# A graph layer's gathers and sums: buffers filled in one direction, sums issued first, one-hots for two parts

## The chip, the cores and the metric

The kernel runs on one core of a Trainium2 chip. The metric is the device time of one execution in microseconds (us). A core has five engines with a queue of instructions each, worked off in order: TensorE (PE, with its weight loads as PEld), VectorE (DVE), ScalarE (ACT), GpSimd (POOL) and SyncE (SP). DMAs are issued from the queues of SP, ACT and POOL. A gather of rows by a list of indices (an indirect DMA) is issued here by POOL.

## The reference

A graph of 12500 nodes with 128 features and 200000 edges, sorted by the edge's target `dst`. Each edge has one of ten relations, the position of the greatest of ten of its attributes. Two layers are computed; the second has no ReLU, and the result is added to `x` and normalized by row.

```python
seg = dst * NUM_REL + edge_type
xs = x[src]
sums = segment_sum(xs, seg, num_segments=N * NUM_REL)
cnt = segment_sum(ones, seg, num_segments=N * NUM_REL)
mean = (sums / maximum(cnt, 1.0)[:, None]).reshape(N, NUM_REL, -1)
return einsum('nrd,rdo->no', mean, w_rel) + x @ root + bias
```

`edge_type = argmax(edge_attr[:, 16:26])`, `h = relu(layer(x))`, `out = layernorm(x + layer(h))`.

## The kernel before

**Tiles and parts.** The edges are cut into 1563 tiles of 128. Four tiles are a *part* (`QB` = 4); layer 1 has 391 parts. For each tile POOL gathers the 128 source rows (`gathered`, L825, the issue is L827). VectorE makes a one-hot matrix of 120 columns (`hots`, L830, L834): 12 nodes that the tile's edges can reach times ten relations, each edge's entry weighted by one over its count. PE multiplies rows and one-hot (`products`, L1063, L1070) into a PSUM bank; two tiles share a bank, and there are four banks (`fixed`). VectorE adds the bank's part of a tile to `cc` at an offset that is read into registers (`sum_into`, L857, the addition is L860). `cc` is a ring of 1024 nodes and an edge of 172; when the tiles cross its end, at tiles 10, 138, 266 and so on (every 128), ACT copies the edge to the front (`lap_begun`, L806 to L808).

**Both layers at once.** From tile 177 (`NX`) on, a gather takes two rows' worth for each edge from the table `TB`: the source's features and, if that node's first layer is already finished and written to `TB`, its projected row for layer 2 (`limit_of` says up to which node). Such a tile has a second product against a *node one-hot* of 12 columns without the relations (L1074). These node one-hots are made in `hots` as well, for the part's four tiles together: an equality into PSUM (`nodeP`, L838) and a product with the weights into the part's one-hot buffer (L840), each over 48 columns. Tiles before 177 are *plain*. What layer 1 could not take along is gathered in layer 2 (L1396), 177 tiles of the early edges and 687 of the later ones, which are brought together in lists on VectorE first.

**Buffers.** Six gather buffers of eight slots of 128 columns. Plain tiles take one slot, two parts to a buffer, and go round six buffers, after tile 48 round five. The others take two slots, a part to a buffer, round four (`NEAR`). Each time that a buffer is used again it is filled in the other direction (`turn`, L1048 to L1051): the slot filled first is then the one whose product ran last. The one-hots go round four buffers (`OB`), made one part ahead (`AHEAD`); the sums of a part come two parts behind its products (`BEHIND`).

**The order.** Layer 1 is written out by hand: each engine gets its instructions in the order of the loop at L1034. Iteration p issues:

1. VectorE: the one-hots of part p+1, the node one-hots among them;
2. POOL: the gathers of part p;
3. VectorE: the sums of tiles 0 and 1 of part p-2 (`sums(0, 2)`, L1077). If the part begins a group of 128 tiles, ACT first fetches a row of offsets by a DMA (L1085); if it begins a group of 16, VectorE loads 16 offsets into registers (L851);
4. PE: the products of tiles 0 and 1 of part p;
5. postponed work that is due (`todo.run`, L1107; `jobs.run`, L1108);
6. VectorE: the sums of tiles 2 and 3 of part p-2, with `lap_begun` on ACT where a lap begins, and then, where a block of nodes has all its edges, `finish` (L918): 20 matmuls that project the block by ten relations (`projected`, L820);
7. PE: the products of tiles 2 and 3, and once more `todo.run`.

`finish` puts its later steps into `todo`: one step later ACT takes the projection out of PSUM (`rows_copied`, L933, the instruction is L749), then the second layer's projections for each relation are made and written to `TB`, and the ring is cleared. `jobs` holds what the later tiles need: for each chunk of 128 tiles the relations, keys and weights (`prepared`, L651), the shifted indices (`shifted_rows`, L435, which also fills `nodeE` for the node one-hots), and the limits of the lists of layer 2: `tile_limits` (L475) runs 252 small instructions (L486), eight at a time, each next eight 8 tiles later, beginning at tile 320.

**The start.** ACT zeroes `cc` in pieces of 512 columns (L1128) while the first chunk is prepared; POOL gathers the first 48 tiles meanwhile.

Of the kernel before, what the change touches and what calls it, by code (L numbers as in the profile page):

```python
# [70 lines left out]
def rgcn_resnorm_kernel(ctx: ExitStack, tc: tile.TileContext, x, src, dst, attr, w_rel1, root1, b1,  # L71
# [145 lines left out]
    gathers = [lasting.tile([P, GQ * C], F32, name=f"g{i}") for i in range(GB)]  # L217
    hots_ = [lasting.tile([P, QB * KY], F32, name=f"oh{i}") for i in range(OB)]
    turn_of_ = {"g": 0, "oh": 0, "ys": 0}

# [113 lines left out]
    iotaP, riotaP, topP, kpP = in_bank(KW), in_bank(NREL), [in_bank(Q), in_bank(Q)], in_bank(P + 2 * L)  # L334
    nodeP = in_bank(QB * WN)
    nc.vector.tensor_copy(iotaP, columns[:, :KW])
# [98 lines left out]
    def shifted_rows(a, b, limit):  # L435

        first = NX // QB * QB if a == NX else a
# [37 lines left out]
    def tile_limits():  # L475
# [7 lines left out]
        for to, first in zip(reach_of, (low_of, high_of)):  # L483
            nc.vector.memset(to, 0.0)
            for i, t in enumerate(first):
                nc.vector.scalar_tensor_tensor(to, u, t - 0.5, to, op0=ALU.is_gt, op1=ALU.add)  # L486
                if i % 8 == 7:
                    yield 1
# [215 lines left out]

    zero = const.tile([P, YB], F32, name="zero")

# [122 lines left out]

    def hots(keys, weights, cols, n, m, nodes=None):  # L830

        oh = next_of("oh", hots_)
        for j in range(n):
            nc.vector.tensor_scalar(oh[:, j * m:(j + 1) * m], cols[:, :m], keys[:, j:j + 1], weights[:, j:j + 1],  # L834
                                    op0=ALU.is_equal, op1=ALU.mult)
        if nodes is not None:
            eq = nodeP[:, :n * WN].rearrange("p (t n) -> p t n", n=WN)
            nc.vector.tensor_tensor(eq, nodes[:, :, None].to_broadcast([P, n, WN]),  # L838
                                    cols[:, None, :WN].to_broadcast([P, n, WN]), op=ALU.is_equal)
            nc.vector.tensor_tensor(oh[:, QB * KW:QB * KW + n * WN].rearrange("p (t n) -> p t n", n=WN), eq,  # L840
                                    weights[:, :, None].to_broadcast([P, n, WN]), op=ALU.mult)
        return oh
# [61 lines left out]
    def layer_1():  # L904
# [118 lines left out]
        for n, a in enumerate(range(0, T0, 2 * G)):  # L1023
            jobs.at((92 + 2 * n) * QB, lambda t, a=a: by_relation(a, min(T0, a + 2 * G)))
        for i, a in enumerate(range(0, RW, YB)):
            def wipe(t, a=a):
                m = min(YB, RW - a)
# [3 lines left out]
        used = {}  # L1031
        turn_of_["zp"] = 0
        fixed = [ps_z.tile([P, YB], F32, name=f"zp{i}") for i in range(4)]
        for p in range(-AHEAD, NPT + BEHIND):  # L1034
            if p + AHEAD < NPT:
                t0, n = parts[p + AHEAD]
                ohs[p + AHEAD] = hots(keyE[:, t0:t0 + n], wE[:, t0:t0 + n], iotaP, n, KW,
                                       nodeE[:, t0 % NODES:t0 % NODES + n] if t0 + n > NX else None)
            if p < 0:
                continue  # L1040
            t = p * QB
            if p < NPT:
                t0, n = parts[p]
                plain = t0 + n <= NX
                if not plain or p % 2 == 0:
                    g = next_of("g", (gathers if t < GB * GQ else gathers[:-1]) if plain else gathers[:NEAR])
                if not plain or p % 2 == 0:
                    turn = used[id(g)] = 1 - used.get(id(g), 1)  # L1048
                slot = [p % 2 * QB + j if plain else 2 * j for j in range(n)]
                if turn:  # L1050
                    slot = [GQ - (1 if plain else 2) - a for a in slot]  # L1051
                for j in range(n):
# [4 lines left out]
                    else:  # L1057
                        gathered(g, slot[j], TB[:N + NREL * limit_of(i)], idx, 2)
                made = (g, ohs.pop(p), slot)
            if p == NPT - CP // 4:  # L1060
                xbs[NBLK - 1] = rows_in(NBLK - 1)
                fTs[NBLK - 1] = features_in(NBLK - 1, 0, xbs[NBLK - 1])
            def products(g, oh, slot, a, b):  # L1063
                n = parts[p][1]
                for j in range(a, min(b, n)):
# [6 lines left out]
                    if i >= NX:  # L1072
                        a = QB * KW + j * WN
                        nc.tensor.matmul(zp[:, o + KW:o + KY], g[:, (slot[j] + 1) * C:(slot[j] + 2) * C], oh[:, a:a + WN],  # L1074
                                         start=True, stop=True)

            def sums(a, b):  # L1077
                nonlocal done, offs, row
                q = p - BEHIND
                if q < 0:  # L1080
                    return
                t0, n = parts[q]
                if not a and t0 % CT == 0:
                    row = rows_.tile([1, CT], I32, name="row")
                    nc.scalar.dma_start(row, b_r[t0 // CT:t0 // CT + 1, :])  # L1085
                if not a and t0 % G == 0:
                    m = min(G, NT - t0)
                    offs = offsets(row[:, t0 % CT:t0 % CT + m], t0, m, bounds)
                for j in range(a, min(b, n)):
                    i = t0 + j  # L1090
                    if i and lap_of_tile(i) > lap_of_tile(i - 1):
                        lap_begun()
                        if lap_of_tile(i) * RN < lap:
                            todo.at(t + 3 * QB, lambda _: edge_cleared())
                    sum_into(NS if i >= NX else NREL, zps[q, j // 2], j % 2 * KY, offs[i % G], WN)
                    if j % 2 or j == n - 1:
                        del zps[q, j // 2]
                if b < QB:
                    return
                while done < NBLK and t0 + n >= done_after(done):  # L1100
                    finish(done, t)
                    done += 1

            if p < NPT - 1:
                sums(0, 2)
                products(*made, 0, 2)
                todo.run(t - QB // 2)  # L1107
                jobs.run(t)  # L1108
                sums(2, QB)
                products(*made, 2, QB)  # L1110
            else:
                jobs.run(t)
                sums(0, QB)
                if p < NPT:
# [10 lines left out]
    flat = cc[:, :NREL].rearrange("p r n -> p (r n)")  # L1125
    for a in range(0, NREL * RW, YB):
        m = min(NREL * RW - a, YB)
        nc.scalar.activation(flat[:, a:a + m], zero[:, :m], AF.Copy)  # L1128
# [603 lines left out]
```

## Time and profile before

| | us |
|---|---|
| median of 3 runs | 3123.92 |
| lowest and highest | 3121.44, 3126.94 |
| the profiled execution, its own time | 3128.32 |
| its span in the profile | 3126.5 |
| busy: PE, DVE, ACT, POOL | 2155.1, 2118.9, 370.3, 2296.7 |
| issue of the first and of the last gather | 4.1, 3105.8 |

The span runs from the first instruction to the end of the last; the execution's own time is a little longer. Busy time of POOL is that of its instructions; a gather's data arrive later than its instruction ends. In a timeline each row has a start, a duration, the engine, the line, and in square brackets the engine's idle time ahead of it with what ended it. In a table of waits, a row tells who waited for whom: the sum in us, how often, the longest.

### The profile page before, as it was taken

How to read it: one execution, taken by the hardware profiler on the slowest of the kernel's cores; microseconds unless marked ns; L12 is line 12 of the kernel's file. 1: busy time of each engine (PE TensorE's matmuls, PEld its weight loads, DVE VectorE, ACT ScalarE, POOL GpSimd, SP SyncE). 2: the span in 40 equal slices, each digit the busy share in tenths (PEclk: the TensorE clock that was granted, in tenths of full speed). 3: DMA queues.
4: the chain of work that ended last, by engine and by line, in shares of the span. 5: the costliest groups of instructions: out<-in, count | busy, mean ns of one | idle time of the engine just before them, and what ended most of it. 6: DMA issues, size and time to landing. Idle time of an engine off the chain costs nothing.

```text
span 3126.5 us, 37701 instructions
## 1 busy us (share of the span) xinstructions
PE 2155.1 (69%) x10120; PEld 1783.0 (57%) x10120; DVE 2118.9 (68%) x8089; ACT 370.3 (12%) x602; POOL 2296.7 (73%) x2439
## 2 busy tenths in 40 slices
PE   2768787877878787888888888843655555555554
PEld 1546666666767676767676767743554444444443
DVE  6868688888777877777776868479773443434443
ACT  1112111111111111111111111100000000000000
POOL 6777777676777777777777777777777777777775
PEclk8778777776878777777777868855755555555555
DMA  6676667575666666666666655532222222222222
GB/s 183 184 216 185 200 184 232 160 215 158 200 193 196 197 194 197 196 196 196 196 185 192 184 159 146 142 94 60 60 60 63 66 70 66 67 66 70 66 67 56
DMA packets 444103, 454.59 MB, mean 145 GB/s; under 512 B 53110, under 2 KB 376239, under 8 KB 443880
## 3 DMA queue, kind: packets, MB, share of 16 engines
q0 software_dynamic: 99840, 250.04, 28.9%
q1 hardware_dynamic: 303331, 182.87, 19.6%
q10 hardware_dynamic: 40709, 19.15, 2.1%
q8 instruction: 85, 1.39, 0.2%
q14 instruction: 138, 1.13, 0.1%
HBM read 309.45 MB, written 148.80 MB: 147 GB/s over the span
## 4 chain that ended last, share of the span: by engine, by line
DVE 30%; POOL 20%; PE 19%; issue 15%; DMA 11%; DVEq 3%; ACT 1%; SPq 0%; POOLq 0%; ACTq 0%
POOL g L827 20%; DVE oh L834 8%; DVE cc L860 7%; PE pf L820 7%; DMA g<-TB,idxE 5%; PE zp L1070 4%; DVEq L851 3%; DMA g<-TB,idxB 2%; PE yb L949 2%; DMA row<-b_r 2%; PE zp L1074 2%; DVE bank L838 1%; DVE reach L486 1%; DVE acc L1554 1%; DVE cc L1274 1%
## 5 line engine op out<-in xcount | busy, mean ns | idle before, releaser
L827 POOL DMA_INDIRECT g<-TB,idxE x1563 | 1478.6, 946 | 525.8 <-issue 421.2
L1070 PE MATMUL zp<-oh,g 128*128 128x120 f32 x3126 | 822.6, 361 | 367.0 <-DVE cc L860 258.3
L1070 PEld LDWEIGHTS zp<-oh,g 128*128 128x128 f32 x3126 | 601.8, 235 | 523.9 <-DVE cc L860 354.5
L827 POOL DMA_INDIRECT g<-TB,idxB x687 | 649.1, 945 | 209.3 <-issue 199.0
L860 DVE TENSOR_TENSOR cc<-cc,zp 128x132 f32 (+1 forms) x1563 | 453.0, 290 | 373.5 <-PE zp L1074 140.7
L1529 PE MATMUL zy<-oh,g 128*128 128x12 f32 (+23 forms) x1170 | 320.3, 380 | 314.0 <-DMA g<-TB,idxB 211.5
L1074 PEld LDWEIGHTS zp<-oh,g 128*128 128x128 f32 x2772 | 529.7, 238 | 0.0
L834 DVE TENSOR_SCALAR oh<-bank,keyE,wE 128x120 f32<-128x120 f32 x1563 | 517.1, 392 | 0.0
L1529 PEld LDWEIGHTS zy<-oh,g 128*128 128x128 f32 x1170 | 274.3, 310 | 370.4 <-DMA g<-TB,idxB 230.5
L1074 PE MATMUL zp<-oh,g 128*128 128x12 f32 x2772 | 481.6, 249 | 0.0
L820 PE MATMUL pf<-cc,w 128*128 128x256 f32 (+2 forms) x1040 | 306.9, 466 | 6.3 <-DVE cc L860 5.9
L949 PE MATMUL yb<-w,a 128*128 128x512 f32 (+1 forms) x576 | 288.2, 583 | 2.3 <-ACT g L955 1.2
L820 PEld LDWEIGHTS pf<-cc,w 128*128 128x128 f32 x1040 | 250.1, 255 | 55.2 <-issue 5.8
L1529 PE MATMUL zq<-oh,g 128*128 128x16 f32 (+27 forms) x558 | 168.1, 395 | 155.6 <-DMA g<-TB,idxB 141.4
L1529 PEld LDWEIGHTS zq<-oh,g 128*128 128x128 f32 x558 | 138.2, 314 | 188.6 <-DMA g<-TB,idxB 154.2
L827 POOL DMA_INDIRECT g<-in_x_dram,idxE x177 | 167.4, 946 | 74.3 <-issue 50.6
L777 DVE TENSOR_TENSOR cc<-pf,cc 128x256 f32<-128x256 f32 (+2 forms) x52 | 21.2, 409 | 264.4 <-PE pf L1472 264.3
L1554 DVE TENSOR_TENSOR acc<-acc,zy 128x12 f32 (+25 forms) x585 | 104.3, 178 | 105.3 <-PE zy L1529 50.7
L834 DVE TENSOR_SCALAR oh<-columns,keyB,wB 128x15 f32<-128x15 f32 (+25 forms) x687 | 163.8, 322 | 0.1
L783 ACT ACTIVATE rstd<-mv,eps 128x2 f32<-128x2 f32 (+2 forms) x52 | 15.3, 295 | 967.1 <-DVE mv L781 967.0
L749 ACT ACTIVATE a<-pf,b 128x256 f32<-128x256 f32 (+1 forms) x50 | 23.3, 466 | 852.9 <-PE pf L822 852.9
L800 ACT ACTIVATE cc<-zero 128x1280 f32<-128x1280 f32 x90 | 118.8, 1368 | 4.8 <-DVE acc L942 4.8
(265 smaller groups left out, 1807.3 us busy)
## 6 DMA issues: line engine op xcount, KB each, us to landing
TB<-xb SPq DMA_DIRECT2D x88, 640.0 KB
m<-in_edge_attr_dram SPq DMA_DIRECT2D x48, 672.0 KB
TB<-g SPq DMA_DIRECT2D x98, 256.0 KB
g<-TB,idxE POOLq DMA_INDIRECT x1563
TB<-ys SPq DMA_DIRECT2D x96, 256.0 KB
g<-TB,idxB POOLq DMA_INDIRECT x687
TB<-ys SPq DMA_DIRECT2D x49, 128.0 KB
TB<-in_x_dram ACTq DMA_DIRECT2D x12, 512.0 KB
```

The costliest lines, as they stand in the source:

```text
L486: nc.vector.scalar_tensor_tensor(to, u, t - 0.5, to, op0=ALU.is_gt, op1=ALU.add)
L800: nc.scalar.activation(cc[:, r, o:o + n], zero[:, None, :n].to_broadcast([P, m, n]), AF.Copy)
L820: nc.tensor.matmul(po[:, :n], wsb[l][:, r, :], sums[:, r], start=(r == 0), stop=(w is None and r == NREL - 1))
L827: nc.gpsimd.indirect_dma_start(out=g[:, j * C:(j + n) * C], out_offset=None, in_=table, in_offset=bass.IndirectOffsetOnAxis(ap=idx, axis=0))
L834: nc.vector.tensor_scalar(oh[:, j * m:(j + 1) * m], cols[:, :m], keys[:, j:j + 1], weights[:, j:j + 1], op0=ALU.is_equal, op1=ALU.mult)
L851: vals = nc.values_load_multi_w_load_instructions(row, engines=[DVE], min_val=min(a for a, _ in lims), max_val=max(b for _, b in lims), sk ...
L860: nc.vector.tensor_tensor(s, s, zp[:, at:at + m * w].rearrange("c (r n) -> c r n", n=w), op=ALU.add)
L949: nc.tensor.matmul(yb[:h, :m], fin_a[k][:, b * P:b * P + h], wsb[1][:, r:r + m // C, :], start=True, stop=True)
L1070: nc.tensor.matmul(zp[:, o:o + KW], g[:, slot[j] * C:(slot[j] + 1) * C], oh[:, j * KW:(j + 1) * KW], start=True, stop=True)
L1074: nc.tensor.matmul(zp[:, o + KW:o + KY], g[:, (slot[j] + 1) * C:(slot[j] + 2) * C], oh[:, a:a + WN], start=True, stop=True)
L1529: nc.tensor.matmul(zp[:, j * w:(j + 1) * w], g[:, at * C:(at + 1) * C], oh[:, j * w:(j + 1) * w], start=True, stop=True)
L1554: nc.vector.tensor_tensor(s, s, zps[q][:, j * w:(j + 1) * w], op=ALU.add)
```

## The change

- Plain buffers are always filled from the front; the alternation stays for the others.
- A part's sums are taken out of the middle of the iteration: tiles 0 and 1 come before the one-hots of part p+1, tiles 2 and 3 between these and the node one-hots, all of them ahead of `todo.run` and `jobs.run`. `finish` stays where it was (`finished`).
- The node one-hots have buffers of their own (`nhots_`, two of 96 columns) and are made for two parts at once, in every other iteration (`node_hots`).
- `tile_limits` issues four instructions at a time, each next four 16 tiles later.
- `zero` has 256 columns instead of 512, and what copies from it takes pieces of 256.

```diff
-    hots_ = [lasting.tile([P, QB * KY], F32, name=f"oh{i}") for i in range(OB)]
+    hots_ = [lasting.tile([P, YB], F32, name=f"oh{i}") for i in range(OB)]
+    nhots_ = [lasting.tile([P, 2 * QB * WN], F32, name=f"nh{i}") for i in range(2)]
...
-                if i % 8 == 7:
+                if i % 4 == 3:
                     yield 1
...
-    zero = const.tile([P, YB], F32, name="zero")
+    zero = const.tile([P, BN], F32, name="zero")
...
+    def node_hots(t0):
+
+        n = min(2 * QB, NT - t0)
+        a = t0 % NODES
+        oh = next_of("nh", nhots_)
+        eq, to = [b[:, :n * WN].rearrange("p (t n) -> p t n", n=WN) for b in (nodeP, oh)]
+        nc.vector.tensor_tensor(eq, nodeE[:, a:a + n, None].to_broadcast([P, n, WN]),
+                                iotaP[:, None, :WN].to_broadcast([P, n, WN]), op=ALU.is_equal)
+        nc.vector.tensor_tensor(to, eq, wE[:, t0:t0 + n, None].to_broadcast([P, n, WN]), op=ALU.mult)
         return oh
...
-        jobs.job(80 * QB, tile_limits(), 2 * QB)
+        jobs.job(80 * QB, tile_limits(), 4 * QB)
...
         for p in range(-AHEAD, NPT + BEHIND):
+            t = p * QB
+            if 0 <= p < NPT - 1:
+                sums(p, t, 0, 2)
             if p + AHEAD < NPT:
                 t0, n = parts[p + AHEAD]
-                ohs[p + AHEAD] = hots(keyE[:, t0:t0 + n], wE[:, t0:t0 + n], iotaP, n, KW,
-                                       nodeE[:, t0 % NODES:t0 % NODES + n] if t0 + n > NX else None)
+                ohs[p + AHEAD] = hots(keyE[:, t0:t0 + n], wE[:, t0:t0 + n], iotaP, n, KW)
+            if 0 <= p < NPT - 1:
+                sums(p, t, 2, QB)
+            if p + AHEAD < NPT and t0 + QB > NX // (2 * QB) * 2 * QB and t0 % (2 * QB) == 0:
+                nhs[(p + AHEAD) // 2] = node_hots(t0)
...
-                if not plain or p % 2 == 0:
+                if not plain:
                     turn = used[id(g)] = 1 - used.get(id(g), 1)
-                slot = [p % 2 * QB + j if plain else 2 * j for j in range(n)]
-                if turn:
-                    slot = [GQ - (1 if plain else 2) - a for a in slot]
+                slot = [p % 2 * QB + j if plain else 2 * (n - 1 - j if turn else j) for j in range(n)]
...
             if p < NPT - 1:
-                sums(0, 2)
                 products(*made, 0, 2)
                 todo.run(t - QB // 2)
                 jobs.run(t)
-                sums(2, QB)
+                finished(p, t)
                 products(*made, 2, QB)
...
-    for a in range(0, NREL * RW, YB):
-        m = min(NREL * RW - a, YB)
+    for a in range(0, NREL * RW, BN):
+        m = min(NREL * RW - a, BN)
         nc.scalar.activation(flat[:, a:a + m], zero[:, :m], AF.Copy)
```

More of the change, by code (lines that the diff above doesn't have):

```diff
@@ L435, in shifted_rows @@
     def shifted_rows(a, b, limit):
-        first = NX // QB * QB if a == NX else a
+        first = NX // (2 * QB) * 2 * QB if a == NX else a
         m, f, _ = relations_of(first, b)
@@ L828, in gathered, with hots @@
                                      in_offset=bass.IndirectOffsetOnAxis(ap=idx, axis=0))
-    def hots(keys, weights, cols, n, m, nodes=None):
+    def hots(keys, weights, cols, n, m):
         oh = next_of("oh", hots_)
@@ L835, in hots @@
                                     op0=ALU.is_equal, op1=ALU.mult)
[L836 to L841, printed above, removed]
+        return oh
+    def node_hots(t0):
[6 more added lines that the diff above has]
+        nc.vector.tensor_tensor(to, eq, wE[:, t0:t0 + n, None].to_broadcast([P, n, WN]), op=ALU.mult)
         return oh
@@ L1059, in layer_1 @@
                 made = (g, ohs.pop(p), slot)
+                nh = nhs.get(p // 2)
             if p == NPT - CP // 4:
@@ L1072, in products @@
                     if i >= NX:
-                        a = QB * KW + j * WN
-                        nc.tensor.matmul(zp[:, o + KW:o + KY], g[:, (slot[j] + 1) * C:(slot[j] + 2) * C], oh[:, a:a + WN],
+                        a = (i % (2 * QB)) * WN
+                        nc.tensor.matmul(zp[:, o + KW:o + KY], g[:, (slot[j] + 1) * C:(slot[j] + 2) * C], nh[:, a:a + WN],
                                          start=True, stop=True)
[L1077 to L1102, printed above, removed]
             if p < NPT - 1:
-                sums(0, 2)
                 products(*made, 0, 2)
@@ L1112, in layer_1 @@
                 jobs.run(t)
-                sums(0, QB)
+                sums(p, t, 0, QB)
+                finished(p, t)
                 if p < NPT:
```

38 lines of the change are left out of this document (33 added, 5 removed).

## The prediction, made before the changed kernel ran

> **What bounds the kernel now.** I read the page first, then the table of busy time by stage, then in the stage that loses time the waits and the groups of VectorE (DVE), and last the timeline around single stalls.
>
> ```profile
> span 3126.5 us, 37701 instructions
> L827 POOL DMA_INDIRECT g<-TB,idxE x1563 | 1478.6, 946 | 525.8 <-issue 421.2
> ```
>
> Every gather is one POOL instruction of 946 ns with an idle stretch before it that nothing ends ("issue"). There are 1563 in layer 1 and 864 in layer 2, 2427 in all, one after another on one queue. Whether that queue is the bound is read from the stages (columns: window, length, then busy time and count of PE, PEld, DVE, ACT, POOL, then clock, DMA share, GB/s):
>
> ```profile
> 50.00:100.00 50.00, 16.89 (x58) 12.98 (x58) 42.29 (x154) 1.49 (x3) 23.63 (x26) 0.50 0.48 141
> ...
> 350.00:800.00 450.00, 348.65 (x1765) 290.10 (x1765) 371.15 (x1458) 72.72 (x106) 313.11 (x332) 0.75 0.64 190
> 800.00:1700.00 900.00, 742.66 (x3835) 626.92 (x3836) 686.55 (x2475) 155.44 (x228) 679.28 (x719) 0.77 0.66 195
> 1700.00:1750.00 50.00, 40.98 (x210) 33.31 (x211) 42.66 (x140) 7.75 (x13) 33.90 (x36) 0.80 0.56 160
> ...
> 1850.00:1950.00 100.00, 87.43 (x448) 70.51 (x448) 79.15 (x279) 18.01 (x27) 72.91 (x78) 0.81 0.50 140
> 1950.00:2050.00 100.00, 74.00 (x452) 63.70 (x452) 47.76 (x179) 15.36 (x35) 73.35 (x79) 0.83 0.56 153
> 2050.00:3100.00 1050.00, 545.19 (x1952) 447.36 (x1953) 552.74 (x2390) 20.77 (x66) 794.07 (x841) 0.52 0.26 65
> ```
>
> In the last row POOL issues 841 gathers in 1050 us, 1.249 us each, and its busy share is 794.07/1050 = 0.756. I take that share as the floor of a stage in which POOL never waits; busy time divided by 0.756 is the time that the stage's gathers need, and the rest of the window is lost. By this the windows lose: 50 to 100: 50 - 31.2 = **18.8**; 350 to 800: 450 - 414 = **36**; 800 to 1700: 900 - 898 = **1.8**; 1700 to 1750: **5.2**; 1850 to 1950: **3.6**; 1950 to 2050: **3.0** us. The sum, 68, is all that a change that leaves the gathers as they are can win: layer 2 and two thirds of layer 1 already run at POOL's pace.
>
> Who holds POOL up between 350 and 800 us:
>
> ```profile
> PE zp L1070 <- DVE cc L860: 87.4, 65, 6.5
> ...
> POOL g L827 <- PE zp L1074: 36.6, 17, 7.6
> ```
>
> A gather waits for the products that last read its buffer; the products wait for VectorE's sums (L860), which empty the PSUM banks. PE is idle for 450 - 348.65 = 101 us there, and 87 of them are that wait. So VectorE is the bound of this stage. Its groups in the window (count | busy, mean ns | idle before):
>
> ```profile
> L834 DVE TENSOR_SCALAR oh<-bank,keyE,wE 128x120 f32<-128x120 f32 x328 | 108.2, 392 | 0.0
> L860 DVE TENSOR_TENSOR cc<-cc,zp 128x132 f32 x329 | 95.8, 291 | 55.5 <-issue 25.2 <-ACT cc L808 6.9 <-PE zp L1074 6.4
> L486 DVE SCALAR_TENSOR_TENSOR reach<-u,reach 128x6 f32<-128x6 f32 x252 | 42.2, 167 | 7.6
> ...
> L838 DVE TENSOR_TENSOR bank<-nodeE,bank 128x48 f32<-128x48 f32 x82 | 17.4, 213 | 2.8
> L840 DVE TENSOR_TENSOR oh<-bank,wE 128x48 f32<-128x48 f32 x82 | 17.0, 207 | 2.8
> ```
>
> All 252 instructions of the list limits (L486) fall into this window, 49.8 us with their gaps, more than the 36 us that POOL loses.
>
> **The change part by part.**
>
> *List limits at a quarter of the pace.* Eight per 8 tiles become four per 16. In this window tiles 320 to about 617 pass: 297/16 = 18.6 steps of 4 instructions of 167 + 30 = 197 ns are 14.6 us in place of 49.8: -35.2. The other 35 us go to tiles 617 to 1344.
>
> *Node one-hots for two parts at once.* Two instructions over 96 columns replace four over 48. No row shows 96, so the price comes from two groups of the same operation:
>
> ```profile
> L860 DVE TENSOR_TENSOR cc<-cc,zp 128x132 f32 x1386 | 404.1, 292 | 336.4 <-PE zp L1074 139.0 <-issue 107.3 <-ACT cc L808 30.8
> ...
> L1554 DVE TENSOR_TENSOR acc<-acc,zy 128x12 f32 x177 | 29.4, 166 | 7.8 <-issue 1.4 <-PE zq L1529 0.7 <-DVE acc L1554 0.6
> ```
>
> (292 - 166)/120 = 1.05 ns a column, so 48 more cost 50 ns: 262 and 257 ns. The bounds are 212 (columns cost nothing) and 424 (no saving); I take the slope. Here 82 pairs of instructions (34.4 busy + 5.6 idle = 40.0 us) become 41 of 262 + 257 + 68 ns of gaps, 24.1 us: -15.9.
>
> *Sums ahead.* This has three effects. First, at a lap's turn:
>
> ```profile
> 1694.72 0.48 ACT L749 ACTIVATE a<-pf,b 128x256 f32<-128x256 f32 x1 [17.28 <-PE pf L822]
> 1695.10 1.77 ACT L808 ACTIVATE cc<-cc 128x1892 f32<-128x1892 f32 x1
> ```
>
> ```profile
> 222.43 0.59 DVE L860 TENSOR_TENSOR cc<-cc,zp 128x120 f32 x2 [7.33 <-ACT cc L808]
> ...
> 379.24 0.62 DVE L860 TENSOR_TENSOR cc<-cc,zp 128x132 f32 x2 [6.91 <-ACT cc L808]
> ...
> 890.23 0.62 DVE L860 TENSOR_TENSOR cc<-cc,zp 128x132 f32 x2 [0.84 <-ACT cc L808]
> ...
> 1696.90 0.62 DVE L860 TENSOR_TENSOR cc<-cc,zp 128x132 f32 x2 [6.72 <-ACT cc L808]
> ...
> 1860.63 0.62 DVE L860 TENSOR_TENSOR cc<-cc,zp 128x132 f32 x2 [7.03 <-ACT cc L808]
> ```
>
> The copy of the ring's edge (L808) stands on ACT behind L749, which waits for the 20 matmuls of a block's projection; the next sum waits for the copy. The four long waits are the laps at which a block ends in the part just before (tiles 136, 264, 1288, 1416). Once the sums of a part are issued ahead of the postponed work, L808 stands ahead of L749 and the projection is no longer in this chain; 0.84 us, as at the lap of 890 us where no block interferes, should stay. The stalls that end at 379, 1697 and 1861 us stand just before or in the windows in which POOL loses.
>
> Second, the row of offsets, once per 128 tiles:
>
> ```profile
> 1027.10 0.50 ACTq L1085 DMA_DIRECT2D row<-b_r  x1
> ...
> 1029.54 1.33 DVE L834 TENSOR_SCALAR oh<-bank,keyE,wE 128x120 f32<-128x120 f32 x4
> ...
> 1035.43 0.62 DVE L860 TENSOR_TENSOR cc<-cc,zp 128x132 f32 x2 [4.08 <-issue]
> ```
>
> ```profile
> 1027.10 5.87 DMA row<-b_r
> ```
>
> The row takes 5.87 us and VectorE has the one-hots (1.8 us, from 1029.54) to do meanwhile. Now it meets the wait first, with those one-hots queued behind it and PE behind the one-hots: a **loss**, bounded by 0 (ACT issues earlier) and 1.8 us a row. I take 1.8: three rows in this window, +5.4. The Trainium skill, "DMA: Bandwidth & Descriptors", section "Latency and other measured facts", puts a DMA's fixed cost at about 2 us, mostly the trip to memory, which the section says shrinks when the memory is lightly loaded. By that estimate the row would have landed at 1029.1, before VectorE comes, and the term would be 0; the 5.87 us row contradicts it here.
>
> Third, a part's sums no longer stand behind the jobs of the same iteration, so PE gets its second bank sooner. I count this at nothing; it is cover for the loss just named.
>
> VectorE's balance from 350 to 800 us: 450 - 35.2 - 15.9 - 6.1 (lap) + 5.4 = 398 us, under the 414 that POOL needs. So POOL becomes the bound here too. What stays lost is bounded by 0.8 us (the rate of 800 to 1700) and 36 (no effect). Busy VectorE time is 371.2 less 29.8 (178 of the 252 limits at 167 ns) less 13.1 (34.4 to 41 x 0.519) = 328 in 414 us, 79%, against 686.55/900 = 76% in the better stage; so I take 6, near the better stage: **-30**.
>
> *Plain buffers in one direction.* The start:
>
> ```profile
> 73.67 0.59 DVE L860 TENSOR_TENSOR cc<-cc,zp 128x120 f32 x2 [5.11 <-issue]
> ...
> 74.31 1.21 PE L1070 MATMUL zp<-oh,g 128*128 128x120 f32 x4 [23.30 <-DVE cc L860]
> ...
> 81.65 1.21 PE L1070 MATMUL zp<-oh,g 128*128 128x120 f32 x4 [1.52 <-DVE cc L860]
> ...
> 83.14 0.94 POOL L827 DMA_INDIRECT g<-in_x_dram,idxE  x1 [19.06 <-PE zp L1070]
> ```
>
> Gather 48 is the first that reuses a buffer, that of tiles 8 to 15. Filled from the other end, it takes tile 15's slot first and waits for the product that runs at 81.65 (tiles 14 and 15). Filled from the front it needs tile 8's, at 74.31: 8.9 us earlier, and each later slot has been read by the time that POOL comes to it at 1.25 us a gather, while PE takes two tiles in 1.7 to 2.9 us. Hoped 8.9, at worst 0 if VectorE cannot keep up with the earlier gathers; the lap stall before 222 us goes, which gives it 6.5 us back, so I take **-8.5**.
>
> *Late stages.* 1700 to 1750 and 1850 to 1950 keep 0.8 us each of 5.2 and 3.6: **-7.2**. From 800 to 1700 the list limits add 45 x 4 x 0.197 = 35.5 us, the nodes take 91 x 0.39 = 35.5 away, and six rows cost 10.8: POOL's loss goes from 1.8 to 4, **+2.2** (bounds: -1.8 and +26, 5.6 rounds at the worst price of the first rival). Layer 2 is not touched: 0.
>
> *Zeroing in halves* doubles ACT's instructions at the start; they end by 16.3 us and ACT then has nothing to do:
>
> ```profile
> 10.16 6.07 ACT L1128 ACTIVATE cc<-zero 128x512 f32<-128x512 f32 x12 [1.76 <-issue]
> 46.01 0.38 ACT L733 ACTIVATE fT<-pf 128x256 f32<-128x256 f32 x1 [29.78 <-PE pf L732]
> ```
>
> Nothing; twice the time would still be hidden in the 29.8 us.
>
> **Sum**: -30 - 8.5 - 7.2 + 2.2 = -43.5. The profiled execution took 3128.32 us (span 3126.5), which gives 3084.8. The median of the runs, 3123.92, is 4.4 lower: **3080**.
>
> **Rivals.**
> 1. *The peaks move on.* In every round of 128 tiles the row wait and the slower list limits put 1.8 + 2.8 us on VectorE before the ring of gather buffers is fullest (some 56 tiles in, 3.5 steps of 0.79) and the nodes take 2.7 off. That is 1.9 us a round, or 4.6 if the wider one-hots save nothing. If the early sums give nothing back, each of eight rounds from 350 to 1700 loses some 3 us: 24 less gain, 3104. For it: POOL's 1.8 us show that the ring is just full today. Against it: the third effect.
> 2. *PE holds the heavy stage.* It is busy 348.65 of 450 us. Then only the start, the laps and the late stages are won, 8.5 + 5 + 7.2: 3103. Against it: 87 of PE's 101 idle us are waits for VectorE.
> 3. *Slower.* VectorE now stands at the head of every part before the sums, with 1.33 us of one-hots behind them that it did before while PE finished. It waited for PE 86.3 us in 180 parts from 800 to 1700:
>
> ```profile
> DVE cc L860 <- PE zp L1074: 86.3, 46, 4.6
> DVE cc L860 <- issue: 62.5, 31, 6.5
> ```
>
> That is 0.48 us a part which can be absorbed, and perhaps 0.14 more, so a part that meets the new wait loses 0.71. It takes 61 of layer 1's 347 later parts to eat the gain; one part in three gives 82 - 43.5, about 3162. Against it: only 46 waits in 180 parts, and they come when VectorE is ahead.
> 4. *Nothing comes of it*: the earlier start is given back and rivals 1 and 2 act together: 3122.
>
> **How the numbers follow.** Forecast (3066 to 3092) 0.62; rival 1 0.20; rival 2 0.08; rival 3 0.06; rival 4 0.04. The low end is all of 36 + 8.8 + 1.8 + 8.9 us won: 3068, and 2 for the scatter of runs. The high end takes in rivals 1 and 2: 3106. About 0.2%, 6 us, is what a measurement here can tell from no change: faster 0.90, same 0.04, slower 0.06.
>
> **What would show it.** Gather 48 at 74 to 75 us; POOL near 0.756 busy from 350 on; L838 and L840 gone, two groups of 173 at about 260 ns in their place; list limits spread to about 1700 us; no wait of some 7 us for L808; the row's wait grown from 4 to about 6 us. If VectorE waits for PE in far more parts, rival 3 is at work; if POOL's waits return every 160 us, rival 1.

## The result and the profile after

The changed kernel takes 3092.51 us (median of 4 runs, 3089.70 to 3093.74), the kernel before in the same group 3123.75 us (4 runs, 3121.44 to 3126.94): a ratio of 0.9898, 95% interval 0.9881 to 0.9915. The forecast was 3080 (3066 to 3106, with 3066 to 3092 for the prediction's own account). The profiled execution after took 3089.7 us.

The page of the kernel after, and its table of busy time by stage (columns as before). The gathers cost what they cost before; the lines have moved: the gather is now L828, the one-hot L835, the sum L866, the copy of the ring's edge L809, the product L1111 and the product with the node one-hots L1115.

```profile
span 3087.4 us, 37680 instructions
L828 POOL DMA_INDIRECT g<-TB,idxE x1563 | 1478.3, 946 | 497.4 <-issue 420.6
```

```profile
50.00:100.00 50.00, 15.81 (x57) 12.75 (x58) 41.15 (x145) 1.86 (x5) 31.10 (x34) 0.50 0.48 144
...
250.00:350.00 100.00, 83.42 (x464) 71.18 (x463) 72.48 (x262) 19.62 (x30) 73.61 (x78) 0.83 0.67 196
350.00:800.00 450.00, 366.04 (x1902) 311.53 (x1901) 342.96 (x1261) 77.13 (x112) 334.86 (x355) 0.76 0.69 204
800.00:1700.00 900.00, 741.10 (x3829) 636.25 (x3828) 679.72 (x2491) 155.31 (x227) 676.19 (x716) 0.75 0.66 194
1700.00:1750.00 50.00, 45.09 (x258) 37.73 (x256) 37.44 (x133) 9.79 (x16) 37.84 (x40) 0.86 0.62 179
1850.00:1950.00 100.00, 89.63 (x504) 75.85 (x505) 64.09 (x225) 15.26 (x30) 75.63 (x80) 0.84 0.53 148
1950.00:2050.00 100.00, 64.64 (x342) 55.24 (x340) 57.93 (x188) 13.23 (x34) 72.28 (x76) 0.69 0.45 119
2050.00:3060.00 1010.00, 521.18 (x1845) 425.96 (x1845) 516.61 (x2291) 17.52 (x54) 763.59 (x809) 0.52 0.26 65
```

The last row is again the pace of an undisturbed POOL: 763.59/1010 = 0.756. Read with it as in the prediction (window less POOL's busy time over 0.756), POOL loses, beside what the forecast left it:

| window, us | before | forecast | after |
|---|---|---|---|
| 50 to 100 | 18.8 | 10.3 | 8.9 |
| 250 to 350 | 0 | 0 | 2.6 |
| 350 to 800 | 36 | 6 | 7.1 |
| 800 to 1700 | 1.8 | 4 | 5.6 |
| 1700 to 1750 | 5.2 | 0.8 | 0 |
| 1850 to 1950 | 3.6 | 0.8 | 0 |
| 1950 to 2050 | 3.0 | 3.0 | 4.4 |

The losses sum to 28.6 us against 68.4 before: 39.8 less, and the spans differ by 39.1. So the whole gain is POOL's lost time coming back.

Where VectorE was the bound, from 350 to 800 us, its groups after are these (count | busy, mean ns | idle before):

```profile
L866 DVE TENSOR_TENSOR cc<-cc,zp 128x132 f32 x358 | 103.1, 288 | 91.8 <-PE zp L1115 60.8 <-issue 22.3 <-ACT cc L809 1.8
...
L487 DVE SCALAR_TENSOR_TENSOR reach<-u,reach 128x6 f32<-128x6 f32 x76 | 12.8, 169 | 2.0
L847 DVE TENSOR_TENSOR nh<-bank,wE 128x96 f32<-128x96 f32 x44 | 11.3, 258 | 1.5
L845 DVE TENSOR_TENSOR bank<-nodeE,bank 128x96 f32<-128x96 f32 x44 | 11.2, 255 | 0.0
```

Of the 252 list limits only 76 are left in the stage. Ninety-six columns cost 255 ns (L845, the equality) and 258 ns (L847, the product with the weights), where 48 cost 213 and 207: 48 columns more cost 42 and 51 ns. The sums run as before. VectorE's idle time ahead of the sums has turned round: 60.8 of 91.8 us is now waiting for PE, where it was 6.4 of 55.5. Its opposite, PE waiting for the sums, is in the table of waits of the same window (sum in us, times, longest):

```profile
PE zp L1111 <- DVE cc L866: 33.6, 21, 3.7
```

```profile
POOL g L828 <- PE zp L1115: 11.6, 14, 5.4
```

21 waits instead of 65, 33.6 us instead of 87.4, and POOL's waits for the products are 11.6 us instead of 36.6. (Each of POOL's 14 contains the usual 0.3 us between two gathers, so 7.4 us of them are loss.)

The start, and two of the places where POOL still loses:

```profile
71.58 0.59 DVE L866 TENSOR_TENSOR cc<-cc,zp 128x120 f32 x2 [4.92 <-issue]
```

```profile
73.28 0.94 POOL L828 DMA_INDIRECT g<-in_x_dram,idxE  x1 [9.14 <-PE zp L1111]
...
541.85 0.94 POOL L828 DMA_INDIRECT g<-TB,idxE  x1 [5.41 <-PE zp L1115]
...
1349.16 0.94 POOL L828 DMA_INDIRECT g<-TB,idxE  x1 [2.56 <-PE zp L1115]
```

The first sum starts at 71.58 instead of 73.67 us, and gather 48 at 73.28 instead of 83.14 us. The other two gathers shown are 416 and 1056. Between 350 and 1700 us POOL loses at the gathers 416, 544, 672 and so on to 1184, and nearly nowhere else: 128 apart, always 32 tiles into a group of 128. How such a loss comes about is seen some 34 us earlier, in the timeline of 1314 to 1353 us:

```profile
1317.97 0.28 DVE L287 CAST idxE<-pf 128x128 int32<-128x128 f32 x1
...
1324.09 0.62 DVE L866 TENSOR_TENSOR cc<-cc,zp 128x132 f32 x2 [5.83 <-PE pf L989]
...
1324.62 1.33 DVE L835 TENSOR_SCALAR oh<-bank,keyE,wE 128x120 f32<-128x120 f32 x4
1324.76 0.50 PEld L1111 LDWEIGHTS zp<-oh,g 128*128 128x128 f32 x2 [1.18 <-DVE cc L866]
...
1330.76 0.78 PE L1111 MATMUL zp<-oh,g 128*128 128x120 f32 x2 [2.35 <-DVE cc L866]
```

```profile
1340.35 7.31 PE L821 MATMUL pf<-cc,w 128*128 128x256 f32 x20
```

VectorE reaches the sums of the group's first part at 1318.2 and sits idle for 5.83 us. The view names PE, but the chain of waits, followed back, has the row of offsets, fetched at 1315.34:

```profile
1315.34 6.03 DMA row<-b_r
1321.40 2.50 DVEq L857
```

The row lands at 1321.37, the register load takes it until 1323.90, and the sum starts at 1324.09. The one-hots of the next part, 1.33 us of VectorE, come only then, and whatever else VectorE has to do comes behind them, the later sums too. PE waits for sums, which empty its banks: 0.78 us at 1324.76 and 2.35 us at 1330.76. It is the same in the whole stretch from 350 to 1700 us, where PE's weight loads for the products wait 127.2 us for sums and 4.8 us for one-hots (sum in us, times, longest):

```profile
PEld zp L1111 <- DVE cc L866: 127.2, 102, 3.8
...
PEld zp L1111 <- DVE oh L835: 4.8, 12, 2.2
```

PE is still behind when it has to run a block's 20 matmuls (7.31 us, at 1340.35), and gather 1056 then waits for a product.

The wait itself is not new. At the six rows between 800 and 1700 us VectorE waited 4.08 to 6.54 us before, 5.4 in the mean, and it waits 3.67 to 6.37 us after, 5.3 in the mean. What the change has altered is the work that stands behind it.

### The profile page after: what moved, and what is told of

Its sections match the earlier page's. It is cut to its first block, busy times and chain, and to the rows that moved or that the text cites. A ratio compares the mean times of both kernels' runs of the same rounds, so it can differ in the third digit from the quotient of the medians.

```text
span 3087.4 us, 37680 instructions
## 1 busy us (share of the span) xinstructions
PE 2139.3 (69%) x10120; PEld 1791.1 (58%) x10120; DVE 2037.7 (66%) x7743; ACT 373.7 (12%) x627; POOL 2296.0 (74%) x2439
## 4 chain that ended last, share of the span: by engine, by line
DVE 25%; POOL 22%; PE 20%; issue 16%; DMA 13%; DVEq 3%; ACT 1%; SPq 0%; POOLq 0%; ACTq 0%
POOL g L828 22%; DMA g<-TB,idxE 7%; DVE oh L835 6%; PE pf L821 6%; PE zp L1111 6%; DVE cc L866 5%; DVEq L857 3%; DMA g<-TB,idxB 3%; PE zp L1115 2%; DMA row<-b_r 2%; PE yb L955 2%; DVE acc L1568 1%; DVE cc L1288 1%; PE pf L1323 1%; DVE eqb L618 1%
## 5 line engine op out<-in xcount | busy, mean ns | idle before, releaser
L828 POOL DMA_INDIRECT g<-TB,idxE x1563 | 1478.3, 946 | 497.4 <-issue 420.6
L1111 PE MATMUL zp<-oh,g 128*128 128x120 f32 x3126 | 818.8, 360 | 329.1 <-DVE cc L866 169.6
L1111 PEld LDWEIGHTS zp<-oh,g 128*128 128x128 f32 x3126 | 609.9, 237 | 460.9 <-DVE cc L866 228.1
L828 POOL DMA_INDIRECT g<-TB,idxB x687 | 648.7, 944 | 209.4 <-issue 197.8
L866 DVE TENSOR_TENSOR cc<-cc,zp 128x132 f32 (+1 forms) x1563 | 448.7, 287 | 438.7 <-PE zp L1115 281.8
L1115 PEld LDWEIGHTS zp<-nh,g 128*128 128x128 f32 x2772 | 534.0, 239 | 0.0
L835 DVE TENSOR_SCALAR oh<-bank,keyE,wE 128x120 f32<-128x120 f32 x1563 | 519.2, 394 | 0.0
L1115 PE MATMUL zp<-nh,g 128*128 128x12 f32 x2772 | 484.4, 250 | 0.0
L828 POOL DMA_INDIRECT g<-in_x_dram,idxE x177 | 167.4, 946 | 64.5 <-issue 35.4
L1568 DVE TENSOR_TENSOR acc<-acc,zy 128x12 f32 (+25 forms) x585 | 104.7, 179 | 108.3 <-PE zy L1543 51.3
L835 DVE TENSOR_SCALAR oh<-columns,keyB,wB 128x15 f32<-128x15 f32 (+25 forms) x687 | 163.7, 324 | 0.0
```

The source lines that it names most:

```text
L828: nc.gpsimd.indirect_dma_start(out=g[:, j * C:(j + n) * C], out_offset=None, in_=table, in_offset=bass.IndirectOffsetOnAxis(ap=idx, axis=0))
L866: nc.vector.tensor_tensor(s, s, zp[:, at:at + m * w].rearrange("c (r n) -> c r n", n=w), op=ALU.add)
L1111: nc.tensor.matmul(zp[:, o:o + KW], g[:, slot[j] * C:(slot[j] + 1) * C], oh[:, j * KW:(j + 1) * KW], start=True, stop=True)
L1568: nc.vector.tensor_tensor(s, s, zps[q][:, j * w:(j + 1) * w], op=ALU.add)
```

## The experiments

In all of them "the changed kernel" is the kernel after. The kernel before took 3780.33 us during the first group of four, 3130.75 us during the second, on the same chip, and 3820.66 us during the third, on another; what differs there is shown in the last section, and only kernels of one group are set beside one another.

**First group: one part undone each.** The sums back in the middle of the iteration (`u_order`, `u_order2`):

```diff
-            if 0 <= p < NPT - 1:
-                sums(p, t, 0, 2)
...
-            if 0 <= p < NPT - 1:
-                sums(p, t, 2, QB)
...
             if p < NPT - 1:
+                sums(p, t, 0, 2)
                 products(*made, 0, 2)
                 todo.run(t - QB // 2)
                 jobs.run(t)
+                sums(p, t, 2, QB)
                 finished(p, t)
```

The list limits at the old pace (`u_limits`, `u_limits2`):

```diff
-                if i % 4 == 3:
+                if i % 8 == 7:
...
-        jobs.job(80 * QB, tile_limits(), 4 * QB)
+        jobs.job(80 * QB, tile_limits(), 2 * QB)
```

Plain buffers alternating (`u_plain`, `u_plain2`) and node one-hots for one part (`u_nodes`, `u_nodes2`):

```diff
-                if not plain:
+                if not plain or p % 2 == 0:
                     turn = used[id(g)] = 1 - used.get(id(g), 1)
-                slot = [p % 2 * QB + j if plain else 2 * (n - 1 - j if turn else j) for j in range(n)]
+                slot = [p % 2 * QB + j if plain else 2 * j for j in range(n)]
+                if turn:
+                    slot = [GQ - (1 if plain else 2) - a for a in slot]
```

```diff
-        n = min(2 * QB, NT - t0)
+        n = min(QB, NT - t0)
...
-            if p + AHEAD < NPT and t0 + QB > NX // (2 * QB) * 2 * QB and t0 % (2 * QB) == 0:
+            if p + AHEAD < NPT and t0 + QB > NX // (2 * QB) * 2 * QB:
```

> The changed kernel with the sums back in their old places (tiles 0 and 1 after the gathers, tiles 2 and 3 behind the postponed work); all else stays. Theory (the early sums matter at the four laps where the edge copy stood behind a projection, and little else): the waits of about 7 us for the edge copy return four times, and POOL loses about 14 us more around 400, 1700 and 1880 us; the row's wait on VectorE goes back from 5.8 to 4 us; about 3105 us against 3092.5 with the change. Rival (the order counts in every part, because PE waited for the sums 345 us in layer 1 before and less now): 3115 or more, POOL's loss spread over the whole layer. Second rival (the longer row wait makes the early sums a loss): 3085 or less.

> The changed kernel with the list limits back at eight instructions per 8 tiles. Theory (VectorE's load between 350 and 800 us was the bound): POOL loses some 20 us more there, about 3110 us, and the small losses of 1 to 2 us at every 128 tiles after 800 us shrink, because no list limits run there. Rival (the early sums and wider one-hots gave VectorE enough room by themselves): 3098 or less.

> The changed kernel with the plain buffers filled in alternating directions as before. Theory: gather 48 waits for tile 15's product again, 8 to 9 us later, of which 3.5 us come back because the first tiles after 177 no longer find the ring full: about 3098 us. Rival (all of the earlier start was given back later, VectorE sets the pace up to 350 us): 3092.

> The changed kernel with the node one-hots made for each part by itself, 48 columns at a time, in the same place behind the sums. VectorE gets about 0.37 us a pair of parts of work back, some 60 us over layer 1. Theory (POOL is the bound now almost everywhere, VectorE has room): the losses at every 128 tiles grow from 1 to 2 us to some 2 to 3 us, and a few us appear between 350 and 800 us: about 3100 us. Rival (VectorE is still as good as the bound): 3110 or more. Second rival (nothing to be seen): 3092.

Measured, in this order: 3758.29 us (ratio to before 0.9932, 0.9912 to 0.9952), 3761.0 (0.9931, 0.9907 to 0.9955), 3771.9 (0.9972, 0.9958 to 0.9987), 3766.62 (0.9956, 0.9938 to 0.9975). These ratios are not exactly those of the two medians. The times expected were thought for a kernel before of 3124 us and say nothing here; the changed kernel itself was not in the group, so no part can be priced by it. All four are between 0.3 and 0.7% faster than before.

**Second group: the changed kernel, the row, the limits, the order.** `ref_after` is the changed kernel again. `e_row` fetches the row of offsets half a group ahead:

```diff
+        ahead_rows = []
+
+        def fetched(c):
+            r = rows_.tile([1, CT], I32, name="row")
+            nc.scalar.dma_start(r, b_r[c:c + 1, :])
+            ahead_rows.append(r)
...
             if not a and t0 % CT == 0:
-                row = rows_.tile([1, CT], I32, name="row")
-                nc.scalar.dma_start(row, b_r[t0 // CT:t0 // CT + 1, :])
+                if t0 == 0:
+                    fetched(0)
+                row = ahead_rows.pop()
+            if not a and t0 % CT == CT // 2 and t0 // CT + 1 < NCH:
+                fetched(t0 // CT + 1)
```

> The changed kernel once more, unaltered, as the mark for the other kernels on the same chip. Where before takes about 3124 us I expect 3091 (ratio 0.990), where before takes about 3780 us, as in the first four kernels, the theory expects less than its 1%: POOL waits there for something else than the parts that were changed, so I expect 3755 (ratio 0.993), about the mean of the four kernels with one part undone; the rival, that the parts add up there as well, expects 3745 (ratio 0.990, below all four).

> The row of offsets is fetched 64 tiles ahead, the rest is the changed kernel. Theory: POOL's remaining losses at the gathers 416, 544, 672 and so on begin with VectorE's wait of some 6 us for the row, so without this wait they fall from 13.1 us between 350 and 1700 us to 0 to 3: 8 to 13 us less than the changed kernel (ratio 0.9957 to 0.9975 to it). Rival: the 20 matmuls of a block's projection, 7 us of PE in the same 128 tiles, cause these losses by themselves; then nothing changes (within 2 us). In either case no VectorE sum is to wait over 1 us for the row.

> The changed kernel with the list limits at the old pace (eight for each 8 tiles). Theory: VectorE's balance from 350 to 800 us goes from 398 back to 433 us against the 414 that POOL needs, so POOL loses some 19 us more there: 12 to 20 us slower than the changed kernel on a chip where before takes 3124 us (ratio 1.004 to 1.0065). Rival: the sums issued ahead alone give VectorE enough room; then within 3 us of the changed kernel. On a chip where before takes 3780 us: within 5 us of the changed kernel.

> The changed kernel with the sums back in the middle of the iteration. Theory: the waits of 7 us for the edge's copy come back (five of them, 6 us each) and PE gets its second bank late, but VectorE has some 16 us of room from 350 to 800 us: 3 to 12 us slower than the changed kernel (ratio 1.001 to 1.004). Rival: the sums ahead cost as much by the wait for the row as they win at the laps; then within 3 us, or faster. On a chip where before takes 3780 us: within 5 us of the changed kernel.

| kernel | median us (lowest to highest) | ratio to before | 95% interval |
|---|---|---|---|
| `ref_after` | 3093.96 (3092.16 to 3095.53) | 0.9881 | 0.9865 to 0.9897 |
| `e_row` | 3084.10 (3081.32 to 3085.88) | 0.9850 | 0.9834 to 0.9866 |
| `u_limits2` | 3105.55 (3101.63 to 3109.20) | 0.9922 | 0.9908 to 0.9936 |
| `u_order2` | 3087.15 (3085.13 to 3090.55) | 0.9864 | 0.9848 to 0.9880 |

`ref_after` came as expected for a kernel before of about 3124 us (3091, ratio 0.990). No two of these ranges overlap, but for the lower end of `u_order2` and the upper of `e_row`. What they did to POOL is one row of the waits between 350 and 1700 us each, in the order of the table:

```profile
POOL g L828 <- PE zp L1115: 27.8, 38, 5.2
```

```profile
POOL g L828 <- PE zp L1125: 14.8, 39, 3.2
```

```profile
POOL g L828 <- PE zp L1115: 38.4, 42, 10.4
```

```profile
POOL g L828 <- PE zp L1111: 13.8, 31, 2.3
```

Less 0.3 us for each, POOL loses 16.4, 3.1, 25.8 and 4.5 us there.

*The row ahead: the theory held.* The loss falls by 13.3 us and the time by 9.9 us, within the 8 to 13 expected; some 2 us are lost again at the start, where gather 48 comes at 75.43 instead of 73.26 us. The edit changes nothing that runs before that gather; in this execution VectorE is 2.4 us late from 34.71 us on, behind a DMA, so these 2 us are put down to scatter. In the chain of waits from 500 to 1700 us the row, 3.6% of it in the changed kernel, is gone, and where the same group's first sum waited 5.83 us it now waits 0.85:

```profile
1311.77 0.62 DVE L866 TENSOR_TENSOR cc<-cc,zp 128x132 f32 x2 [0.85 <-PE yb L955]
```

The projections of about 7 us are all still there. By themselves they cost POOL next to nothing after the first round: the rival falls. Of the 3.1 us that are left, 2.9 are at gather 416, whose cause stays open:

```profile
540.06 0.95 POOL L828 DMA_INDIRECT g<-TB,idxE  x1 [3.21 <-PE zp L1125]
```

*The list limits* cost 11.6 us when undone, just under the 12 to 20 expected. The extra loss of POOL is 9.4 us; it comes in the stage that the prediction named (7.5 us from 350 to 800 us grow to 21.1, and part of that is made up for later). Gather 416 alone waits twice as long:

```profile
547.09 0.94 POOL L828 DMA_INDIRECT g<-TB,idxE  x1 [10.35 <-PE zp L1115]
```

*The order: the theory fell, the rival's "or faster" came.* With the sums back in the middle the kernel is **6.8 us faster** than the changed one. Gather 416 shows the same:

```profile
539.27 0.94 POOL L828 DMA_INDIRECT g<-TB,idxE  x1 [1.37 <-PE zp L1111]
```

Its rows still take 5 to 6.3 us each in the chain of waits, and VectorE's wait is as long as ever, 6.42 us at the row fetched at 1310.69 (the timeline, with the one-hots done just before):

```profile
507.05 5.12 DMA row<-b_r
...
1148.04 6.34 DMA row<-b_r
```

```profile
1311.20 1.33 DVE L835 TENSOR_SCALAR oh<-bank,keyE,wE 128x120 f32<-128x120 f32 x4
1318.94 0.62 DVE L866 TENSOR_TENSOR cc<-cc,zp 128x132 f32 x2 [6.42 <-issue]
```

So it isn't that the wait for the row is gone. In this order the next part's one-hots are issued ahead of that wait, and VectorE has done them when the row lands; in the changed kernel they stand behind it, ahead of the later sums. Either cure, the row ahead or the old order, takes away most of the losses at 32 tiles into a group (at gather 416 the row ahead leaves 2.9 us, the old order 1.1). That it is the one-hots' place is argued from the code and these rows: the old order also moves the jobs, and the two were not tried apart. VectorE's waits between 350 and 1700 us, first of the changed kernel, then of `u_order2`:

```profile
DVE cc L866 <- PE zp L1115: 196.3, 94, 5.9
...
DVE cc L866 <- ACT cc L809: 5.4, 9, 0.6
```

```profile
DVE cc L866 <- PE zp L1111: 114.4, 46, 5.5
DVE nh L847 <- PE zp L1111: 73.6, 30, 6.2
...
DVE cc L866 <- ACT cc L809: 12.7, 6, 6.6
```

VectorE's time waiting for PE is nearly the same in sum (196.3 against 114.4 + 73.6 = 188.0 us); only the place differs. The long waits for the edge's copy come back at all four laps at which the prediction saw them:

```profile
219.33 0.59 DVE L866 TENSOR_TENSOR cc<-cc,zp 128x120 f32 x2 [6.21 <-ACT cc L809]
...
372.48 0.62 DVE L866 TENSOR_TENSOR cc<-cc,zp 128x132 f32 x2 [6.63 <-ACT cc L809]
...
1656.40 0.62 DVE L866 TENSOR_TENSOR cc<-cc,zp 128x132 f32 x2 [5.43 <-ACT cc L809]
...
1816.91 0.62 DVE L866 TENSOR_TENSOR cc<-cc,zp 128x132 f32 x2 [6.06 <-ACT cc L809]
```

In the changed kernel each of them is 0.60 us. But POOL pays for only one: after the third lap gather 1340 waits 2.0 us too long, and behind the other three no gather waits over 0.8 us longer than in the changed kernel. So the theory was right about the waits and wrong about their price.

**Third group: the two other parts, the limits alone, and both cures.** `o_limits2` is the kernel before with the new pace of the list limits only (the diff above, the other way round); `e_row_order` joins `e_row` and `u_order`.

> The changed kernel with the plain buffers alternating again. Theory: gather 48 waits for tile 15's product again, some 9 us later than now, but the changed kernel gives 1.5 to 3.5 us of its earlier start back at the gathers 177 to 204, so the net is 5 to 8 us slower than the changed kernel (ratio 1.0016 to 1.0026). Rival: the time won at the start is given back wholly in the first heavy rounds (the losses at gathers 416 and 544 shrink when POOL comes later); then within 2 us.

> The changed kernel with node one-hots for each part by itself (48 columns). Theory: VectorE has 16 us more to do from 350 to 800 us and 35 us more from 800 to 1700 us; by the list limits, where 35 us more cost 11.6, the first costs some 5 and the second at most as much again, because VectorE has slack there: 4 to 12 us slower than the changed kernel (ratio 1.0013 to 1.004). Rival: the pairs for two parts bunch the work before the peaks, so undoing them costs nothing (within 2 us).

> The kernel before with only the list limits' pace changed. Theory: VectorE's 450 us from 350 to 800 us lose 35, which leaves POOL some 10 of its 36 us of loss: 20 to 26 us faster than before (ratio 0.9917 to 0.9936). Rival: the parts hide one another, and alone it is worth the 11.6 us that its undoing cost, or less (ratio 0.996 or more).

> The changed kernel with the row of offsets fetched 64 tiles ahead and the sums back in the middle of the iteration, to be set beside the row fetched ahead with the sums first (3084.1 us). Theory A: the order's only harm was the wait for the row, and its other effects (no 7 us wait for the edge's copy, an earlier second bank) are a gain: 3 to 8 us slower than that kernel. Theory B: the order brings nothing, since the lists and one-hots gave VectorE enough room for the old waits: within 2 us of it. Theory C: VectorE's waits for PE ahead of the one-hots cost by themselves: 3 us or more faster than it.

Measured against a kernel before of 3820.66 us: `u_plain2` 3822.77 (ratio 1.0004, 0.9991 to 1.0017), `u_nodes2` 3822.83 (1.0009, 0.9993 to 1.0025), `o_limits2` 3817.0 (0.9990, 0.9978 to 1.0002), `e_row_order` 3778.36 (0.9886, 0.9867 to 0.9904). Under that condition POOL is not the steady bound (last section), so none of the theories is decided as stated. What the group does show: the kernel with the early row and the old order is the only one of this group that gains, 1.1%; and the two kernels measured in both long-time groups, which ran on two chips, do not agree with themselves beyond their intervals (`u_plain` 0.9972 and 1.0004, `u_nodes` 0.9956 and 1.0009), so ratios from there do not carry over. The prices of the plain buffers' direction and of the node one-hots stay without a timed experiment.

## Why the prediction came out as it did

**What bounds it: right.** The span fell by 39.1 us, and POOL lost 39.8 us less. The time, 3092.5, is 12.5 us above the forecast and half a us above the band (3066 to 3092) that the prediction gave its own account; it lies in the wider range because part of rival 1 came true.

**350 to 800 us, -30: right, measured -28.9.** The list limits are the part that was tested: undoing them costs 11.6 us of time, and 13.6 us of POOL's loss in this stage. What bought the other 15 us there was not tested. The one-hots' slope of 1.05 ns a column gave 262 and 257 ns, and 255 and 258 were measured. What their 15.9 us of VectorE are worth in time was not measured.

**Start, -8.5: measured -9.9, and then 2.6 us given back** between 250 and 350 us, where no loss was before and none was forecast. In the trace these are gathers 191, 192 and 204, which wait 1.17, 1.31 and 1.18 us instead of 0.3. That they wait because POOL comes there earlier than the products do is argued; the experiment meant to show it fell under the other condition.

**Late laps, -7.2: measured -8.8, but not for the reason given.** The copy of the edge no longer stands behind the projection, as forecast. Yet in `u_order2`, where it does again, only 2.0 us of the gain are lost, at gather 1340, so most of it was not bought by the order of the sums, and that the number came out near is luck. Undoing the list limits costs nothing there either (POOL is busy 37.82 and 75.63 us in the two windows of `u_limits2`, at its floor). The node one-hots, or several parts together, are left by elimination; this was not tested.

**Sums ahead: wrong in sign.** The forecast gave this part +6.1 us of VectorE time won at laps, 5.4 lost at rows and a third effect, counted at nothing, as cover for the loss. The lap waits did go, but POOL had paid little for them; the runs show a net cost of 6.8 us. The step that failed is "it is cover for the loss just named": PE's earlier second bank did not cover the row. Of the mechanism of that loss the first half was read rightly, one-hots queued behind the wait. The second half, "PE behind the one-hots", is not what the trace names: PE waits for the sums behind them. Nor did VectorE's wait grow "from 4 to about 6 us", since the one row of 4.08 us that it was read from was the shortest of six. The price is 13.3 us of POOL in eight rounds, 1.7 us a round. That this is near the prediction's 1.8 us a row is chance: those were VectorE's, and the other terms were to absorb them. The row itself took about as long as before (5.3 us in the mean of eight against 5.0); here are the first of all, and then the first and the shortest of the changed kernel's eight between 500 and 1700 us:

```profile
66.69 1.74 DMA row<-b_r
```

```profile
508.43 5.63 DMA row<-b_r
...
1478.25 3.26 DMA row<-b_r
```

The Trainium skill, "DMA: Bandwidth & Descriptors", section "Latency and other measured facts", puts a DMA's fixed cost at about 2 us; by that estimate the row would be there in about 2 us. The trace agrees for the first row, which is fetched while POOL stands still ahead of gather 48 (1.74 us), and not for the eight that are fetched beside the running gathers (3.26 to 6.34 us). That the gathers' traffic makes the difference was not tested. `e_row` shows that the wait for the row is paid for, whatever its length comes from.

**800 to 1700 us, +2.2: right in sign, measured +3.8.** Rival 1 said that losses would return every 160 us; they did, by the first of the two causes that it named, the row's wait; the slower list limits were not needed for it, since `e_row` keeps their pace. Its price of 3 us a round was too high: 12.7 us by the windows are 1.6 a round.

**From the span to the number.** Made against the profiled execution's own time the sum gave 3084.8; after's own time is 3089.7. Of these 4.9 us, 2.6 are the start's give-back, 1.4 the first gathers of layer 2, 2.7 the heavy stage and the one behind it, less 3.0 that the start and the late laps won more; the remaining 1.2 lie outside the table. Of the 12.5 us between 3080 and 3092.5 another 7.2 are scatter: the execution profiled before was 4.4 us above the median of its runs, the one after 2.8 below. The last 0.4 come from rounding 3080.4 to 3080.

**Rivals 2, 3 and 4.** PE does not hold the heavy stage: 366.04 of 450 us busy, POOL 0.744 against a floor of 0.756. VectorE does wait for PE more often (rival 3: 66 waits and 135.5 us from 800 to 1700 where there were 46 and 86.3) without harm, except at the rows: a wait of an engine that has time to spare costs nothing until something else stands behind it. Rival 4, no effect at 3122, lies outside the interval.

```profile
DVE cc L866 <- PE zp L1115: 135.5, 66, 5.9
```

The best version measured is the changed kernel with the row fetched ahead: 3084.1 us, ratio 0.9850 (0.9834 to 0.9866) to before. Whether the old order on top of it is better still was measured under the other condition only.

## What to carry to other kernels

When an instruction that may wait is moved to the head of an in-order queue, price the wait by the work that is queued behind it and by who waits for that, and look whether the operand can be fetched earlier: here one small fetch moved by 64 tiles was worth 9.9 us. And a wait that an edit removes is worth only what the bounding engine paid for it: of four waits of about 6 us on VectorE, POOL had felt one, with 2.0 us. A bundle of edits that gains can hold one that loses; undoing them one at a time on the chip finds it, though not when another bound rules. Work that is due at any time belongs outside the stage that is full.

## What the runs showed of the hardware

The same program on the same chip took 3780 us once and 3131 us later. That was not foreseen, and its cause stays open. The instructions of POOL and VectorE have the same durations in both: a gather 946 to 948 ns, a one-hot 393 and 394 ns. POOL's busy time between 350 and 800 us, however, is 274.74 us in `u_plain2` (third group) where it is 334.86 in the changed kernel; in `u_plain`, on the first group's chip, it is 275.86:

```profile
350.00:800.00 450.00, 327.33 (x1565) 272.86 (x1563) 275.13 (x1003) 61.43 (x91) 274.74 (x291) 0.73 0.57 166
```

What grows is time between instructions that no engine of the profile accounts for ("remote"). POOL itself has 104.2 us of it between 350 and 1700 us, and VectorE this much from 800 to 1700 us, both in `u_plain2`:

```profile
DVE cc L866 <- remote: 164.2, 45, 10.6
```

In layer 2 some sums that follow one another on the same engine start 1.4 us apart there,

```profile
3716.26 0.18 DVE L1570 TENSOR_TENSOR acc<-acc,zq 128x22 f32 x1 [6.45 <-remote]
3717.65 0.18 DVE L1570 TENSOR_TENSOR acc<-acc,zq 128x22 f32 x1 [1.22 <-DVE acc L1570]
```

where the same sums (L1568 there) run four in 0.81 us in `ref_after`:

```profile
3006.57 0.81 DVE L1568 TENSOR_TENSOR acc<-acc,zq 128x23 f32 x4
```

A gain that comes from an engine's own queue can vanish under such a condition, so the kernel before and the kernel after belong in the same group of runs.
